# A convolution whose patches come straight out of the projection, and a scan whose states are added by identity products

## The chip, the core and the metric

The kernel runs on one core of a Trainium2 chip. The core has a matrix engine (PE, with its weight loads shown as PEld), a vector engine (DVE), an activation engine (ACT), a general engine (POOL, GpSimd) and a queueing engine (SP), which work side by side and wait for one another through semaphores; DMA engines move data. The matrix engine's clock is throttled: the profile shows the share of full speed that was granted. The metric is the device time of one execution in microseconds (us), as the median of several runs.

## The reference

Two blocks of a "metaformer" work on x of shape (2, 128, 64, 64), in float32. Each block has a token mixer and a feed-forward part, each on a normed input and with a residual. Block 0 is a deformable convolution (branches of 1x1, 1x1, 3x3, 7x7: 60 taps, each a bilinear gather) and a mixture of 8 experts. Block 1, whose mixer the change is about, is this, and ends in a mixture of 64 experts:

```
xz = einsum('ed,bdhw->behw', in_proj_w, ln_c(x))        # 128 -> 512 channels
xz = depthwise 5x5 convolution of xz, padding 2
x, z = xz[:, :256], xz[:, 256:]                          # 4096 positions each
x = sigmoid(ca(mean(x)) + ca(max(x))) * x                # channel attention
z = sigmoid(conv1d(mean and max of z over channels)) * z # position attention
x = silu(causal depthwise conv1d(x) + bias)
dt, Bm, Cm = parts of x_proj_w @ x
delta = softplus(dt_proj_w @ dt + dt_proj_b)
s[d,n]  = exp(delta*A[d,n]) * s[d,n] + delta*Bm[n]*x[d]  # scan over 4096 positions
y[d]    = sum_n s[d,n] * Cm[n] + D[d]*x[d]
out     = out_proj_w @ (y * silu(z))
```

There are 256 channels d (two halves of 128 partitions) and 16 states n.

## The kernel before, in words

**Stages and order.** On each engine the instructions run in the order in which the program issues them. The program interleaves jobs by hand: each job is a generator, its `yield` is the end of a step, and a `Side` holds a list of generators and advances the first by one step when asked. The stages are: image 0 normed; its 480 (8 groups of 512 positions by 60) gather taps, beside the offset convolutions of both images; the 480 taps of image 1, beside `after(0)`, which is image 0's norm and fusing, its first feed-forward part and its `convs(0)`; then the scan of block 1 over 16 pieces, of which the first 8 (image 0) run beside `after(1)`, the same steps for image 1; and the last feed-forward part. `sample(b, g, ..., pace)` advances the rest stream by `pace` steps per tap (L526). A scan piece is 512 positions, and one *unit* of it is one state of one half, so that a piece has 32 units; each unit advances the rest stream by five steps and a small stream `side` by two (the next piece's `prepare`, and the last one's `project`).

**The convolution, `convs(b)`.** The 512 projected channels are convolved on PE as products of patches with position matrices. The image is cut in 8 x 11 = 88 patches of 8 x 6 positions, each of which needs a halo of two: 12 x 10 = 120 values. `hs` holds the image as 11 strips (`NJ`) of 68 x 10. The steps are these:

- `norm` (L1010): a group of 512 tokens is loaded, normed, transposed on PE to `pb`, copied to `hn` by ACT (L1020) and stored to a buffer `hd` in DRAM on ACT's DMA queue (L1021).
- For each pair of channel blocks (`o`, 64 channels each), `strips` (L1025) loads every group of `hd` again on SP's queue (L1028), multiplies it with the 128 columns `own` of the projection (L1032), and copies the result into `hs` with three ACT copies (L1035, L1039, L1040).
- "ps1": for each block, 88 patches are put on partitions by a PE transpose of 64 channels x 120 positions each (L959), eight to a bank, and copied to `X` by ACT.
- "ps2": for each of the 64 channels, `X` (120 x 88) times the position matrix `tm` (120 x 48) gives the 48 outputs of all patches (L972), copied to `Y`.
- "ps3": 48 transposes (L988) bring channels back to partitions, and ACT copies them to `img`, which is stored to DRAM on SP's queue (`xsd` or `zsd`). For the z half, two reductions of `Y` on DVE (`zst`) feed the position attention.

The ACT copies are held back by two banks (`later`), and so are the stores behind them.

**The scan.** `prepare` (L1117) loads a piece of x (`xc`), of z (`zz`), of the residual (`xr`) and of the position attention (`sab`), at its start, and works out `xs` (x after conv1d), `dl` (delta), `du` (delta times x), the rows `bc` of B and C, and `dx` = D times x (L1217, ACT). For unit u the loop `scan` then runs `drive` (POOL, `db` = du times B, three units ahead, L1246), `decay` (ACT, `da` = exp, two ahead, L1253), the scan instruction (DVE, L1303), `keep` (ACT, saves the last state, L1310) and `sc` = states times C (DVE, L1313). The `sc` tile of a unit is added to `py` (one PSUM bank per half) one unit later, by four accumulating 128x128 PE transposes (L1271), so that `py` has positions on partitions. `fetch` loads the B and C rows of a state, broadcast to all partitions (512 KB), into one of `BCB` = 6 buffers (L1261). At the end of a piece, `project` copies `py` to `yt` (L1337), transposes it back (eight transposes, L104), multiplies with z (L1349), projects (L1354), adds the residual (L1364) and stores.

## Time and profile before

| | us |
|---|---|
| median of 3 runs | 8280.49 |
| lowest and highest | 8272.83, 8282.75 |
| the profiled execution | 8332.4 |
| its span, at a mean clock of 0.80 | 8330.6 |

The profile comes from one execution. Times of single instructions overlap in a pipelined engine, so a busy sum of PE isn't its time at peak. The stages, as the first and last instructions of their lines in the trace show them (us from the start of the span):

| from | to | what runs |
|---|---|---|
| 0 | 198 | norm of image 0 |
| 198 | 3093 | gathers of image 0, offset convolutions |
| 3093 | 6045 | gathers of image 1, beside `after(0)` |
| 6045 | 7435 | scan of image 0, beside `after(1)` |
| 7435 | 8055 | scan of image 1 |
| 8055 | 8330 | last feed-forward part |

The costliest rows of the groups (line, engine, operation, output<-inputs by the program's names, partitions x elements, count; then busy us, mean ns of one, idle us before and what ended it) are the gathers, their weighting and the scan's factors:

```profile
L547 POOL DMA_INDIRECT v<-table,idx x3840 | 3643.7, 949 | 2384.2 <-issue 1000.0
...
L558 DVE TENSOR_TENSOR v<-v,pw 128x1024 f32<-128x1024 f32 x960 | 1169.5, 1218 | 1060.9 <-DMA v<-table,idx 871.0
L568 PE MATMUL pst<-ident,v 128*128 128x128 f32 x7680 | 1240.2, 304 | 823.3 <-issue 529.5
...
L1246 POOL TENSOR_TENSOR db<-du,bcb 128x512 f32<-128x512 f32 x512 | 660.0, 1293 | 937.2 <-DVE da L1303 897.4
...
L1253 ACT ACTIVATE da<-delta,w_A_log 128x512 f32<-128x512 f32 x512 | 354.0, 692 | 17.3 <-DVE delta L1209 1.5
```

### The profile page before, as it was taken

The page shows a single profiled execution, that of the slowest core. Times are in us where ns is not written, and L with a number is a line of the kernel's source. Part 1 is how long each engine was busy: PE and PEld are TensorE (multiplying, and loading weights), DVE is VectorE, ACT ScalarE, POOL GpSimd, SP SyncE. Part 2 cuts the span into 40 slices and gives each one's busy share as a digit, 9 for nine tenths or more (in the row PEclk, how much of TensorE's full clock was granted, in tenths as well). Part 3 has the DMA queues.
Part 4 walks back from the last instruction along what each step waited for, and adds up shares of the span by engine and source line. Part 5 has one row for each costly group of instructions (what it writes and reads, how often), then busy time and mean ns, then how long its engine had stood idle before and what let it go on. Part 6 is the DMA issues. An engine that isn't in the chain of part 4 may idle for free. (4 is left out here: it accounts for less than half of the span.)

```text
span 8330.6 us, 83751 instructions
## 1 busy us (share of the span) xinstructions
PE 5808.5 (70%) x27808; PEld 4000.1 (48%) x27808; DVE 5729.7 (69%) x8508; ACT 2120.9 (25%) x4432; POOL 4590.5 (55%) x4576
## 2 busy tenths in 40 slices
PE   2688888888888867766766676666755565855558
PEld 2456656666666644443434443344434444733335
DVE  1577777777777776777786667666647745669981
ACT  1111111111111113211111221112163344655540
POOL 0456666666666666666666666666534433347640
PEclk7788999999999988888888888788876665656568
DMA  4677666666666668867677777777653344434434
GB/s 128 185 249 216 195 207 203 205 213 197 207 203 206 208 212 261 270 213 234 218 240 203 228 204 223 219 206 216 176 166 135 127 110 107 128 106 149 145 124 141
DMA packets 636007, 1579.35 MB, mean 190 GB/s; under 512 B 167700, under 2 KB 247356, under 8 KB 623036
## 3 DMA queue, kind: packets, MB, share of 16 engines
q0 software_dynamic: 307200, 1006.88, 40.6%
q1 hardware_dynamic: 298284, 515.10, 19.5%
q10 hardware_dynamic: 30096, 52.03, 1.7%
q8 instruction: 226, 3.70, 0.2%
q14 instruction: 201, 1.65, 0.1%
HBM read 1456.11 MB, written 120.01 MB: 189 GB/s over the span
## 5 line engine op out<-in xcount | busy, mean ns | idle before, releaser
L547 POOL DMA_INDIRECT v<-table,idx x3840 | 3643.7, 949 | 2384.2 <-issue 1000.0
L597 PE MATMUL out<-st,regw 128*128 128x512 f32 x3840 | 2115.3, 676 | 161.2 <-issue 108.7
L558 DVE TENSOR_TENSOR v<-v,pw 128x1024 f32<-128x1024 f32 x960 | 1169.5, 1218 | 1060.9 <-DMA v<-table,idx 871.0
L568 PE MATMUL pst<-ident,v 128*128 128x128 f32 x7680 | 1240.2, 304 | 823.3 <-issue 529.5
L577 ACT COPY st<-pst 128x512 f32<-128x512 f32 x960 | 558.3, 585 | 4347.3 <-remote 2367.5
L568 PEld LDWEIGHTS pst<-ident,v 128*128 128x128 f32 x7680 | 1001.1, 157 | 1162.1 <-issue 786.9
L564 DVE TENSOR_TENSOR v<-v,low 128x512 f32<-128x512 f32 x1920 | 1318.0, 686 | 65.4
L563 DVE TENSOR_TENSOR low<-v,pw 128x512 f32<-128x512 f32 x1920 | 1329.0, 692 | 33.4
L1246 POOL TENSOR_TENSOR db<-du,bcb 128x512 f32<-128x512 f32 x512 | 660.0, 1293 | 937.2 <-DVE da L1303 897.4
L597 PEld LDWEIGHTS out<-st,regw 128*128 128x128 f32 x3840 | 762.0, 221 | 776.6 <-issue 713.7
L334 PEld LDWEIGHTS po<-wout,ring 128*128 128x128 f32 x5120 | 740.1, 198 | 366.5 <-issue 365.1
L334 PE MATMUL po<-wout,ring 128*128 128x147 f32 x5120 | 785.6, 299 | 167.4 <-issue 162.3
L1303 DVE TENSOR_TENSOR_SCAN da<-da,state,db 128x512 f32<-128x512 f32 x512 | 657.1, 1283 | 278.3 <-ACT da L1253 260.8
L1271 PE MATMUL py<-ident,sc 128*128 128x128 f32 x2048 | 463.0, 379 | 336.2 <-DVE sc L1313 335.1
L1271 PEld LDWEIGHTS py<-ident,sc 128*128 128x128 f32 x2048 | 338.6, 196 | 476.8 <-DVE sc L1313 441.5
L1313 DVE TENSOR_TENSOR sc<-da,bcb 128x512 f32<-128x512 f32 x512 | 354.2, 692 | 48.6 <-DVE da L1303 1.9
L1253 ACT ACTIVATE da<-delta,w_A_log 128x512 f32<-128x512 f32 x512 | 354.0, 692 | 17.3 <-DVE delta L1209 1.5
L972 PE MATMUL ps<-tm,X 120*88 120x48 f32 x2048 | 246.1, 299 | 62.9 <-ACT Y L924 22.5
L972 PEld LDWEIGHTS ps<-tm,X 120*88 120x88 f32 x2048 | 241.7, 213 | 94.4 <-issue 41.4
L959 PE MATMUL ps<-ident,hs 64*120 64x64 f32 x1408 | 142.1, 271 | 124.9 <-ACT X L924 69.8
L988 PE MATMUL ps<-ident,Y 88*64 88x88 f32 x768 | 108.1, 291 | 155.9 <-ACT img L924 100.1
L959 PEld LDWEIGHTS ps<-ident,hs 64*120 64x120 f32 x1408 | 125.5, 177 | 184.2 <-ACT X L924 89.5
(270 smaller groups left out, 4811.1 us busy)
## 6 DMA issues: line engine op xcount, KB each, us to landing
bcb<-bc SPq DMA_DIRECT2D x256, 512.0 KB
regw<-in_regw SPq DMA_DIRECT2D x66, 1280.0 KB
v<-table,idx POOLq DMA_INDIRECT x3840
yd<-ys ACTq DMA_DIRECT2D x128, 256.0 KB
yc<-yd SPq DMA_DIRECT2D x32, 1024.0 KB
gb<-gd SPq DMA_DIRECT2D x16, 2048.0 KB
wt<-in_weight SPq DMA_DIRECT2D x32, 1024.0 KB
tm<-pos SPq DMA_DIRECT2D x16, 1440.0 KB
```

Source lines behind the costliest of these rows:

```text
L334: m()
L547: nc.gpsimd.indirect_dma_start(out=v[:, j, :], out_offset=None, in_=self.table[b], in_offset=bass.IndirectOffsetOnAxis(ap=idx[:, j, t : t ...
L558: nc.vector.tensor_tensor(up, up, w, ALU.mult)
L563: nc.vector.tensor_tensor(low, v4[:, two, 2:4, :], w, ALU.mult)
L564: nc.vector.tensor_tensor(up[:, two], up[:, two], low, ALU.add)
L568: nc.tensor.matmul(pt[:, j, :], v4[:, j, q, :], env.ident, is_transpose=True, start=j == 0 and q == 0, stop=j == GT - 1 and q == 1,)
L577: nc.scalar.copy(st, pt.rearrange("p j t -> p (j t)"))
L597: nc.tensor.matmul(self.out[half], self.regw[t // CH][:, t % CH, half * P : (half + 1) * P], st, start=first, stop=last,)
L972: nc.tensor.matmul(ps[:, c, :], X[:, c0 + c, :], tm[:, :, c0 + c], start=True, stop=True)
L1246: nc.gpsimd.tensor_tensor(dbs[u], pieces[k]["du"][:, half, :], bcb[u // 2][:, 0, :], ALU.mult)
L1271: nc.tensor.matmul(out[:, j, :], what[:, j * P : (j + 1) * P], env.ident, is_transpose=True, start=first and j == 0, stop=last and j == GT ...
L1303: nc.vector.tensor_tensor_scan(s, s, dbs.pop(u), state[:, half, n : n + 1], ALU.mult, ALU.add)
```

## The change

- `norm` no longer stores to DRAM: it copies the normed, transposed group from PSUM into `hs`, which now holds the 128 normed channels, once per image. `strips` and `hd` are gone.
- ps1 projects while it puts patches on partitions: a patch of `hs` (128 x 120) is the stationary operand, and the block's 64 columns of the projection are the moving one.
- For image 1 two blocks share one `Y`, so that ps3 transposes 88 x 128 and `img` has 128 channels (`yg`).
- `py` keeps channels on partitions: `sc` is added by one product with the identity as stationary operand, issued two units after its own; D times x is a product with a diagonal matrix `dg`, made once, issued at the piece's fourth unit. `project` then needs neither `yt` nor transposes; it runs at the head of `side` from the third unit of the next piece, and loads `xr` itself.
- Six buffers for `sc` in place of five, five for `bcb` in place of six; `zz` and `sab` load six steps later; four rest steps per unit in place of five; two rest steps per tap everywhere in place of three in group 0 of image 1.

```
-                self.sample(1, g, *cur, conv, rest, 2 if g else 3)
+                self.sample(1, g, *cur, conv, rest, 2)
...
-BCB = 6
+BCB = 5
...
-        yield from mixed([self.norm(b, g, sp, bank) for g in range(NG)], 2)
-        zst = sp.tile([NPATCH, 2, 4, NPOS], F32, name="zst", bufs=1)
+        yield from mixed([self.norm(b, g, hs, sp, bank) for g in range(NG)], 2)
+        yg = CG if b == 0 else 2 * CG
+        zst = sp.tile([NPATCH, 2, 256 // yg, NPOS], F32, name="zst", bufs=1)
         for o in range(512 // CG):
-            if o % 2 == 0:
-                own = ipw[:, o * CG : (o + 2) * CG]
-                yield from mixed([self.strips(b, g, own, hs, sp, bank) for g in range(NG)], 2)
+            ch = o * CG % yg
+            if ch == 0:
+                Y = sp.tile([NPATCH, NPOS, yg], F32, name="Y", bufs=1)
...
+            own = ipw[:, o * CG : (o + 1) * CG]
             for p0 in range(0, NPATCH, 8):
                 ps = bank([KP, 8, CG], "ps1")
                 for k in range(8):
                     i, j = divmod(p0 + k, NJ)
-                    nc.tensor.transpose(
-                        ps[:, k, :],
-                        hs[ch, j, PH * i : PH * i + PH + 4, :].rearrange("p y x -> p (y x)"),
-                        env.ident[ch, ch],
-                    )
+                    patch = hs[:, j, PH * i : PH * i + PH + 4, :].rearrange("p y x -> p (y x)")
+                    nc.tensor.matmul(ps[:, k, :], patch, own, start=True, stop=True)
...
+            if ch + CG < yg:
+                continue
...
-                    ps = bank([CG, nx, NPATCH], "ps3")
+                    ps = bank([yg, nx, NPATCH], "ps3")
...
-        nc.scalar.copy(hn, pb)
-        nc.scalar.dma_start(out=self.hd[b][:, g * 512 : (g + 1) * 512], in_=hn.rearrange("p j t -> p (j t)"))
-        yield
-
-    def strips(self, b, g, own, hs, sp, bank):
...
+        yield
+
+        pb = pb.rearrange("p j (y x) -> p (j y) x", x=W)
         rows = slice(2 + 8 * g, 10 + 8 * g)
         nc.scalar.copy(
             hs[:, 1:NJ, rows, 0:PW].rearrange("p j y x -> p y j x"),
...
+        dg = sp.tile([P, 2, P], F32, name="dg", bufs=1)
+        for h in range(2):
+            nc.vector.tensor_scalar(dg[:, h, :], env.ident, self.D[:, h : h + 1], None, ALU.mult)
...
-            for j in range(GT):
-                nc.tensor.matmul(
-                    out[:, j, :],
-                    what[:, j * P : (j + 1) * P],
-                    env.ident,
-                    is_transpose=True,
...
+            nc.tensor.matmul(py[k, half], by, what, start=first, stop=last)
...
-            if n == 0 and half == 0:
-                side.add(tail)
+            if k and n == 1 and half == 0:
+                side.todo.appendleft(project(k - 1))
...
-            sc = sp.tile([P, LC], F32, name="sc", bufs=5)
+            sc = sp.tile([P, LC], F32, name="sc", bufs=6)
...
-            for _ in range(5):
+            for _ in range(4):
                 rest.step()
...
             if n == 0 and half == 0:
-                py.clear()
-                adds.extend((h, now["dx"][:, h, :], True, False) for h in range(2))
-            adds.append((half, sc, False, n == DS - 1))
+                adds.extend((u + 3, k, h, dg[:, h, :], now["xs"][:, h, :], True, False) for h in range(2))
+            adds.append((u + 2, k, half, env.ident, sc, False, n == DS - 1))
+            while adds and adds[0][0] <= u:
+                add(*adds.popleft()[1:])
...
+    def project(self, b, k, py, ys, sp, pp):
+
+        nc = self.env.nc
+        xr = sp.tile([P, GT, C], F32, name="xr", bufs=1)
+        nc.sync.dma_start(out=xr, in_=self.x2[b][:, k * GT : (k + 1) * GT, :])
         for half in range(2):
             y = ys[:, half, :]
-            nc.vector.tensor_tensor(y, y, pts[half].rearrange("p j t -> p (j t)"), ALU.mult)
+            nc.vector.tensor_tensor(y, y, py[half], ALU.mult)
```

More of the change, by code (lines that the diff above doesn't have):

```diff
@@ L900, in __init__ @@
         self.zsd = [self.dp.tile([256, N], F32, name=f"zsd{b}", tag=f"zsd{b}") for b in range(B)]
-        self.hd = [self.dp.tile([P, N], F32, name=f"hd{b}", tag=f"hd{b}") for b in range(B)]
         self.att = [self.dp.tile([2, N + 6], F32, name=f"att{b}", tag=f"att{b}") for b in range(B)]
@@ L953, in convs @@
             X = sp.tile([KP, CG, NPATCH], F32, name="X", bufs=1)
-            ch = slice(o % 2 * CG, (o % 2 + 1) * CG)
+            own = ipw[:, o * CG : (o + 1) * CG]
             for p0 in range(0, NPATCH, 8):
@@ L966, in convs @@
             yield from last()
-            Y = sp.tile([NPATCH, NPOS, CG], F32, name="Y", bufs=1)
             for c0 in range(0, CG, 8):
@@ L974, in convs @@
                     )
-                later(copy(Y[:, :, c0 : c0 + 8], ps.rearrange("p c s -> p s c")))
+                later(copy(Y[:, :, ch + c0 : ch + c0 + 8], ps.rearrange("p c s -> p s c")))
                 yield
             yield from last()
+            if ch + CG < yg:
+                continue
             x_half = o < 4
             for py in range(PH):
-                img = sp.tile([CG, NI, W], F32, name="img", tag="io", bufs=3)
-                ch = slice((o % 4) * CG, (o % 4 + 1) * CG)
+                img = sp.tile([yg, NI, W], F32, name="img", tag="io", bufs=3)
+                at = (o + 1) * CG % 256 or 256
+                ch = slice(at - yg, at)
                 dst = self.xsd[b][ch, 3:] if x_half else self.zsd[b][ch, :]
@@ L998, in convs @@
             if not x_half:
-                nc.vector.tensor_reduce(zst[:, 0, o - 4, :], Y, AX.X, ALU.add)
+                nc.vector.tensor_reduce(zst[:, 0, (o - 4) * CG // yg, :], Y, AX.X, ALU.add)
                 yield
-                nc.vector.tensor_reduce(zst[:, 1, o - 4, :], Y, AX.X, ALU.max)
+                nc.vector.tensor_reduce(zst[:, 1, (o - 4) * CG // yg, :], Y, AX.X, ALU.max)
             yield
@@ L1007, in convs, with norm @@
         yield from self.position_attention(b, zst, sp, bank)
-    def norm(self, b, g, sp, bank):
+    def norm(self, b, g, hs, sp, bank):
         env, nc = self.env, self.env.nc
@@ L1019, in norm @@
         yield
-        nc.scalar.copy(hn, pb)
-        nc.scalar.dma_start(out=self.hd[b][:, g * 512 : (g + 1) * 512], in_=hn.rearrange("p j t -> p (j t)"))
         yield
-    def strips(self, b, g, own, hs, sp, bank):
-        nc = self.env.nc
-        h = sp.tile([P, 512], F32, name="h", tag="io", bufs=3)
-        nc.sync.dma_start(out=h, in_=self.hd[b][:, g * 512 : (g + 1) * 512])
-        for _ in range(3):
-            yield
-        pb = bank([P, 8, W], "pj")
-        nc.tensor.matmul(pb.rearrange("p y x -> p (y x)"), own, h, start=True, stop=True)
-        yield
+        pb = pb.rearrange("p j (y x) -> p (j y) x", x=W)
         rows = slice(2 + 8 * g, 10 + 8 * g)
@@ L1127, in prepare @@
         )
-        zz = sp.tile([P, 2, LC], F32, name="zc")
-        nc.sync.dma_start(out=zz, in_=self.zsd[b].rearrange("(h p) l -> p h l", p=P)[:, :, l0 : l0 + LC])
-        xr = sp.tile([P, GT, C], F32, name="xr")
-        nc.sync.dma_start(out=xr, in_=self.x2[b][:, k * GT : (k + 1) * GT, :])
-        sa = sp.tile([P, LC], F32, name="sab", bufs=1)
-        nc.sync.dma_start(out=sa, in_=self.sad[b][0, l0 : l0 + LC].partition_broadcast(P))
         def gap(n):
@@ L1138, in prepare @@
         yield from gap(6)
+        zz = sp.tile([P, 2, LC], F32, name="zc")
+        nc.sync.dma_start(out=zz, in_=self.zsd[b].rearrange("(h p) l -> p h l", p=P)[:, :, l0 : l0 + LC])
+        sa = sp.tile([P, LC], F32, name="sab", bufs=1)
+        nc.sync.dma_start(out=sa, in_=self.sad[b][0, l0 : l0 + LC].partition_broadcast(P))
         halves = range(2)
@@ L1214, in prepare @@
             yield
-        dx = sp.tile([P, 2, LC], F32, name="dx", bufs=1)
-        for h in halves:
-            nc.scalar.mul(dx[:, h, :], xs[:, h, :], self.D[:, h : h + 1])
-        res.update(dx=dx, zz=zz, dl=dl, du=du, xr=xr)
-        yield
+        res.update(xs=xs, zz=zz, dl=dl, du=du)
     def scan(self, sp, ps, pp, rest, ahead):
@@ L1238, in scan @@
         units = [(k, n, half) for k in range(B * NK) for n in range(DS) for half in range(2)]
-        pieces, das, dbs, bcb, tail = {0: res}, {}, {}, {}, iter(())
+        pieces, das, dbs, bcb = {0: res}, {}, {}, {}
         def drive(u):
@@ L1261, in fetch, with add, project @@
                 nc.sync.dma_start(out=bcb[i], in_=pieces[k]["bc"][n].partition_broadcast(P))
-        adds, py = deque(), []
-        def add(half, what, first, last):
+        adds, py = deque(), {}
+        def add(k, half, by, what, first, last):
             if first:
-                py.append(ps.tile([P, GT, P], F32, name=f"py{half}", tag=f"py{half}", bufs=1))
-            out = py[half]
-            for j in range(GT):
-                nc.tensor.matmul(
-                    out[:, j, :],
-                    what[:, j * P : (j + 1) * P],
-                    env.ident,
-                    is_transpose=True,
-                    start=first and j == 0,
-                    stop=last and j == GT - 1,
-                )
+                py[k, half] = ps.tile([P, LC], F32, name=f"py{half}", tag=f"py{half}", bufs=1)
+            nc.tensor.matmul(py[k, half], by, what, start=first, stop=last)
+        def project(k):
+            return self.project(k // NK, k % NK, [py.pop((k, h)) for h in range(2)], pieces[k]["zz"], sp, pp)
         fetch(BCB - 3)
@@ L1316, in scan @@
                 side.step()
-            for _ in range(5):
+            for _ in range(4):
                 rest.step()
-            while adds:
-                add(*adds.popleft())
             if n == 0 and half == 0:
-                py.clear()
-                adds.extend((h, now["dx"][:, h, :], True, False) for h in range(2))
-            adds.append((half, sc, False, n == DS - 1))
-            if n == DS - 1 and half == 1:
-                add(*adds.popleft())
-                yt = sp.tile([P, 2, GT, P], F32, name="yt", bufs=1)
-                tail = self.project(k // NK, k % NK, tuple(py), yt, now["zz"], now["xr"], pp)
-        for _ in tail:
-            pass
-    def project(self, b, k, py, yt, ys, xr, pp):
-        env, nc = self.env, self.env.nc
+                adds.extend((u + 3, k, h, dg[:, h, :], now["xs"][:, h, :], True, False) for h in range(2))
+            adds.append((u + 2, k, half, env.ident, sc, False, n == DS - 1))
+            while adds and adds[0][0] <= u:
+                add(*adds.popleft()[1:])
+        while adds:
+            add(*adds.popleft()[1:])
+        for _ in project(B * NK - 1):
+            pass
+    def project(self, b, k, py, ys, sp, pp):
+        nc = self.env.nc
+        xr = sp.tile([P, GT, C], F32, name="xr", bufs=1)
+        nc.sync.dma_start(out=xr, in_=self.x2[b][:, k * GT : (k + 1) * GT, :])
         for half in range(2):
-            nc.scalar.copy(yt[:, half, :, :], py[half])
-        yield
-        yield
-        pts = []
-        for half in range(2):
-            pt = pp.tile([P, GT, P], F32, name="pty", tag="m")
-            transpose4(nc, env.ident, pt, [yt[:, half, j, :] for j in range(GT)])
-            pts.append(pt)
+            y = ys[:, half, :]
+            nc.vector.tensor_tensor(y, y, py[half], ALU.mult)
             yield
         yield
-        for half in range(2):
-            y = ys[:, half, :]
-            nc.vector.tensor_tensor(y, y, pts[half].rearrange("p j t -> p (j t)"), ALU.mult)
-            yield
         po = pp.tile([P, GT, P], F32, name="po", tag="m")
```

## The prediction

> **What bounds it now.** I read the slices first, then windows cut at the stage borders (seen where L597, L1303 and L1518 begin and end), then waits and groups of each stage.

> ```profile
> PE   2688888888888867766766676666755565855558
> DVE  1577777777777776777786667666647745669981
> PEclk7788999999999988888888888788876665656568
> ```
> Read down a column: from slice 29 (6045 us) the clock falls to 5–6 tenths, while no engine is over 8 tenths busy until slice 37. The windows (us; busy us of PE, weight loads, DVE, ACT, POOL; clock; DMA share; GB/s) show three stages that the change touches: image 1's gathers (C), the first and the second half of the scan.
> ```profile
> 3093.00:6045.00 2952.00, 2019.78 (x9104) 1242.68 (x9104) 2106.53 (x3015) 571.60 (x1162) 1839.46 (x1936) 0.83 0.73 223
> 6045.00:7435.00 1390.00, 832.13 (x4564) 650.24 (x4564) 824.12 (x1107) 680.17 (x1355) 510.97 (x375) 0.64 0.41 124
> 7435.00:8055.00 620.00, 334.03 (x1337) 222.70 (x1336) 589.69 (x601) 343.96 (x674) 427.06 (x337) 0.60 0.42 142
> ```
> The second half is bound by DVE: 590 of 620. C and the first half have no full engine: instructions of two jobs stand interleaved in each engine's order, and each waits for the other. The waits of the first half (total us, times, longest):
> ```profile
> DVE da L1303 <- ACT da L1253: 260.8, 64, 21.3
> ACT state L1310 <- DVE sc L1313: 147.5, 53, 15.9
> ACT Y L924 <- PE ps L972: 100.0, 43, 11.5
> PE py L1271 <- DVE sc L1313: 81.4, 42, 7.4
> ```
> Here is a ring: the scan waits for ACT's decay, which stands behind copies of conv results; ACT waits for PE, PE waits for the scan's C product, and so back to DVE. So the convolution's PE time, and the add that holds PE, are path. All waits of this stage that end on PE come to some 290 of 1390 us: a fifth, which I use below as the share of spread-out PE time that counts.

> **How much side work each stage takes.** Counting the generators' yields: image 0's side stream has 988 steps now against 1020 offered (60 taps at 3, 420 at 2), so it lasts nearly all of C. After: the strips' 152 steps go, 836 against 960 at 2: it ends near tap 420, some 40 taps earlier than today. Image 1's stream: 1164/5 = 233 units now, 930/4 = 232.5 after: the scan is covered just as long, with 4 steps a unit in place of 5.

> **New patch products (ps1): the largest added cost.** Rows (group: count | busy, mean ns | idle before):
> ```profile
> L959 PE MATMUL ps<-ident,hs 64*120 64x64 f32 x1408 | 142.1, 271 | 124.9 <-ACT X L924 69.8
> L972 PE MATMUL ps<-tm,X 120*88 120x48 f32 x2048 | 246.1, 299 | 62.9 <-ACT Y L924 22.5
> ```
> 1408 = 16 × 88 transposes: one instruction each. L972 is a true f32 product: 1024 in the code, 2048 instructions. So the new 1408 products become 2816 instructions with 128-row loads. Means contain pipeline overlap, so I use spacing of starts: L959 0.059 us at full clock, 0.107 at half; L972 (120x48) 0.085/0.147; a 128x128 load with a short moving side (expert gate, L1518) 0.213 at half. I take 0.105/0.20 for one new instruction, two per patch: 88 × 0.21 = 18.5 us for 64 channels at full clock (35 at half) against 5.2 (9.4). Eight of these per image: **+106 us full, +206 half**.

> **Strips out.** 64 PE instructions of 128x512 (0.43/0.85 us), 96 less 24 ACT copies, 8 stores on ACT's queue and 32 loads on SP's go per image, as does the store-to-load round trip. By where L1032 runs, strips take 378 us of C (68 taps, 5.56 each) and 82 us of the scan's first half (24 units, 3.4 each). The 24 remaining copies go into norm's emptied step; the bank is held a step longer, under transposes that wait on loads anyway.

> **Stage C.** A tap costs 5.0 us by POOL's issue alone (four gathers at 0.95 plus 0.30 between them); 6.15 on average. Strips −378; the 40 bare taps come back at about 5.15 (channel statistics, a stretch with little side work, shows 5.17): +206. The finish of image 0, 60 taps at pace 3, becomes 83 at pace 2: +23 × ~5.2 = +120; norm with the strip copies and what followed the last strip: 4 taps, +21. (23 − 68 + 4 + 40: still 480 taps.) Sum −31. Then ps1: 44 taps at 5.6 today. A tap's own PE work is 2.6 (transposes 0.87, four 128x512 products 1.72); two new ps1 banks add 3.36 at full clock: 5.95, and 11.5 at half. The like stretch, ps2, is 5.3 by the same sum and took 6.85 at a clock of 0.86; so 7.2 is taken, 44 × 1.6 = +70. **C: +39**, from −15 (6.0 a tap) to +100 (8.5, less some).

> **First half.** *Strips* −32: of 82, the 24 units still cost about 2.1 each bare. *ps1*: a block of 64 channels takes 19 us today, PE's own part 7 to 8, the rest waits in the ring. After, PE bounds it: at clock 0.70, 18.5/0.70 = 26.4 us, and 14 steps at four a unit put 3.5 adds of 1.2 us between: 30.5, 8 × 11.5 = **+90**. In the same way +124 at 0.62 (today's), +177 at half, +50 at 0.85, +14 full. *ps2* follows the clock: −12 (+8 at 0.62, −40 at 0.85). *ps3 of image 1* (88x64 transposes become 88x128; 384→192 instructions, copies and DMAs 64→32, bytes unchanged): of 174 us, PE and ACT counts halve, widths don't: −49. *Adds two units later*: today add u stands on PE one unit behind its product, and ps1–ps3 behind it wait those 81 us; later, the product is long done. I take four fifths, −64; ACT's decay is late next, so not all. But an add is longer (below): 0.5 us × 204 units outside ps1 × a fifth = +20. **−44**. The sc tile is held a unit longer and has a buffer more: no new wait of DVE. *Projection*: two yt copies (ACT, 30.9 us of waits), eight pty transposes and two dx scalings per piece go: −20; D·x becomes two 512-column products. **Sum −67**, range −150 to +100.

> **Identity products against transposes[...].**
> ```profile
> L1271 PE MATMUL py<-ident,sc 128*128 128x128 f32 x2048 | 463.0, 379 | 336.2 <-DVE sc L1313 335.1
> L597 PE MATMUL out<-st,regw 128*128 128x512 f32 x3840 | 2115.3, 676 | 161.2 <-issue 108.7
> ```
> An add is four transposes, 4 × 0.109 = 0.44 us full, 0.85 half. L597 shows what it becomes: 960 taps × 2 halves are 1920 products, 3840 instructions, two each. So 0.86 full, 1.7 half. [...] The row's instruction count decides: 1.7 under 2.4, hidden by DVE, **0**. That DVE cover is 1283 + 692 ns a unit: 32 × 1.975 + 14.5 of piece work = 77.7 against 78.4 measured, and the change takes nothing from it. One y multiply per half remains. Second half 0 ± 10.

> [...] The trace is split:
> ```profile
> 6110.00:6232.00 122.00, 88.47 (x312) 57.86 (x312) 45.17 (x53) 90.92 (x179) 27.62 (x22) 0.86 0.58 186
> 7233.00:7254.00 21.00, 20.64 (x136) 20.48 (x136) 6.26 (x7) 6.16 (x14) 2.55 (x2) 0.50 0.01 2
> 8140.00:8166.00 26.00, 26.00 (x122) 25.22 (x121) 3.14 (x6) 3.51 (x6) 0.00 (x0) 0.50 0.00 1
> ```
> Wide true products (first row: 256 columns moved) stood at 0.86; but the second row is dense ps2, true products with 48 columns, and the third dense 64-column ones: both 0.50 with PE full. [...] New adds are wide and new ps1 narrow: hence 0.70.

> **Smaller edits.** BCB 6→5: a C/B row has three units' slack instead of four (about 7 us), against about 4 from issue to landing; POOL's wait on it today is 9 us. zz, sab after six steps: first used units later; xr, loaded in project with one buffer: needed five steps on. SP's queue holds only these and tm, img. Cost 0; if the cover fails, up to 1 us for each of 128 rows.

> **Rivals.**
> (1) *The clock doesn't rise* (slower). ps1's 64-column products run slow like the third row above, beside a scan at 0.60. First half: +124 +8 −32 −49 −20, and adds at half clock −64 + 0.85 × 204 / 5 = −29: +2; C at 7.7 a tap: +61; tail −3: +60, **8340**. It decides when the first half's clock stays below about 0.67. For: dense ps2 at 0.50. Against: the wide adds.
> (2) *It rises to 0.85*: +50 −40 −32 −49 −50 −20 = −141, C −10: **8130**. [...] Against: 0.50.
> (3) *Parts cancel*, clock near 0.67: **8280**.
> (4) *Late prefetch*: 1 us a row in the second half, +128, on −30: **8378**.

> **Numbers.** C +39, first half −67, second 0, tail −3 (shorter last projection): −31. Durations come from an execution of 8332.4 us (span 8330.6), 0.6% over the median of 8280.5; 0.6% of 31 is nothing, so it is taken from the median: **8250**. Chances: forecast 0.38, rival 1 0.36, rival 2 0.08, rival 3 0.13, rival 4 0.05. 0.2% (16.6 us) is what can be told from no change: faster 0.46, same 0.13, slower 0.41. The forecast's own range is 8180 to 8262; with the others 8150 to 8370.

> **What will show it.** Strips (L1032, h loads) gone; ps1 spacing near 0.105/0.20 and two instructions a patch; clock 6045–7435 at 0.70 or more (rival 1: 0.62 or under); PE's wait for sc under 30 us; second half 620 ± 10 with PE near 1.7 a unit[...]; C some 2990 us, with 40 bare taps at its end. The forecast is wrong if C grows over 100 us or the first half doesn't shrink.

## The result, and the profile after

The changed kernel takes 8164.42 us in the median of 4 runs (8158.65 to 8199.58), the kernel before 8278.98 (8272.83 to 8282.75): ratio 0.9871, 95% interval 0.9842 to 0.99. So it is 1.3% faster, some 115 us where 31 were forecast. The profiled execution took 8158.65 us (span 8156.9).

The profiled execution of before took 8332.4 us, 0.6% over its median and longer than any of its timed runs, and part of that lies where the change touches nothing: image 0's taps lasted 2894 us in it and 2867 after. Chips differ in this stretch in the runs below too (2863 to 2872 on one, 2898 to 2912 on the others). So a difference of stage lengths between two traces holds such a part too, and verdicts rest on ratios to the kernel before, run on the same chip.

First the slices of after (a column is 204 us):

```profile
PE   2588888888888875767776886887556677956668
PEclk9789999989999987978888888888777787877788
```

Against the rows shown of before: the clock stands at 7 to 8 tenths from slice 29 on, where it had been 5 to 6. The windows of the three stages (columns as before: us, busy PE, weight loads, DVE, ACT, POOL, clock, DMA, GB/s), and two short ones, the last ps1 block and the last ps2 block of image 1:

```profile
3098.00:5951.00 2853.00, 2027.41 (x9618) 1306.13 (x9616) 2081.71 (x2983) 538.34 (x1068) 1817.12 (x1913) 0.84 0.72 223
6012.00:7267.00 1255.00, 882.91 (x4402) 582.32 (x4402) 807.43 (x1093) 597.38 (x1156) 495.50 (x364) 0.78 0.40 123
7267.00:7881.00 614.00, 406.70 (x728) 137.37 (x728) 588.35 (x599) 329.58 (x643) 425.89 (x337) 0.77 0.43 144
7092.00:7112.00 20.00, 20.00 (x180) 19.03 (x179) 7.06 (x8) 8.64 (x17) 6.89 (x6) 1.00 0.57 153
7113.00:7126.00 13.00, 13.00 (x134) 11.88 (x134) 4.98 (x6) 4.89 (x11) 3.82 (x3) 1.00 0.01 1
```

The taps are taken by their weighting (L558), the scan from one scan instruction (L1303 before, L1286 after) to another. So taken, the stages are:

| | before | after | difference |
|---|---|---|---|
| taps of image 0 (unchanged code) | 2894 | 2867 | −27 |
| taps of image 1 | 2907 | 2853 | −55 |
| scan, first half | 1351 | 1255 | −96 |
| scan, second half | 617 | 613 | −4 |

The first half holds most of it; what image 1's taps are worth is taken up below. Second half and tail are where the prediction put them: PE's busy time went from 334 to 407 us of some 615 in the second half, hidden by DVE. In the first half PE has *more* busy time than before (883 against 827, from the first scan instruction on) in a shorter stage. The last two rows of the fence say how: PE, full in ps1 for 20 us, stood at a clock of 1.00, and so did ps2, which had stood at 0.50 in the same place before. The groups:

```profile
L1258 PE MATMUL py<-sc,ident 128*128 128x512 f32 x1024 | 646.2, 747 | 227.8 <-DVE sc L1296 226.5
...
L962 PE MATMUL ps<-ipw,hs 128*120 128x64 f32 x2816 | 341.8, 285 | 32.7 <-ACT X L924 20.5
...
L970 PE MATMUL ps<-tm,X 120*88 120x48 f32 x2048 | 190.3, 265 | 18.7 <-issue 8.6
```

1408 patches are 2816 instructions and 512 adds 1024: two each, as the prediction had read from rows of before. ps2, which nobody edited, went from 246 to 190 us busy in the whole kernel.

### The profile page after: what moved, and what is told of

It reads as the page before. It is cut to its first block, busy times and chain, and to the rows that moved or that the text cites. A ratio compares the mean times of both kernels' runs of the same rounds, so it can differ in the third digit from the quotient of the medians.

```text
span 8156.9 us, 82968 instructions
## 1 busy us (share of the span) xinstructions
PE 5965.2 (73%) x27680; PEld 3939.3 (48%) x27680; DVE 5724.5 (70%) x8506; ACT 2015.3 (25%) x4142; POOL 4590.3 (56%) x4576
## 5 line engine op out<-in xcount | busy, mean ns | idle before, releaser
L597 PE MATMUL out<-st,regw 128*128 128x512 f32 x3840 | 2076.0, 665 | 137.9 <-issue 78.8
L558 DVE TENSOR_TENSOR v<-v,pw 128x1024 f32<-128x1024 f32 x960 | 1169.2, 1218 | 1039.7 <-DMA v<-table,idx 850.7
L568 PE MATMUL pst<-ident,v 128*128 128x128 f32 x7680 | 1219.1, 302 | 753.6 <-issue 404.4
L597 PEld LDWEIGHTS out<-st,regw 128*128 128x128 f32 x3840 | 750.8, 218 | 741.5 <-issue 666.3
L334 PE MATMUL po<-wout,ring 128*128 128x147 f32 x5120 | 802.8, 301 | 218.3 <-issue 215.5
L1286 DVE TENSOR_TENSOR_SCAN da<-da,state,db 128x512 f32<-128x512 f32 x512 | 656.8, 1283 | 239.9 <-ACT da L1242 232.1
L1258 PE MATMUL py<-sc,ident 128*128 128x512 f32 x1024 | 646.2, 747 | 227.8 <-DVE sc L1296 226.5
L1258 PEld LDWEIGHTS py<-sc,ident 128*128 128x128 f32 x1024 | 200.2, 224 | 553.8 <-DVE sc L1296 422.8
L962 PEld LDWEIGHTS ps<-ipw,hs 128*120 128x120 f32 x2816 | 342.1, 202 | 79.2 <-ACT X L924 39.3
L962 PE MATMUL ps<-ipw,hs 128*120 128x64 f32 x2816 | 341.8, 285 | 32.7 <-ACT X L924 20.5
L970 PEld LDWEIGHTS ps<-tm,X 120*88 120x88 f32 x2048 | 185.9, 168 | 52.9 <-issue 26.3
L334 PE MATMUL po<-wring,ring 128*128 128x174 f32 x1024 | 187.4, 323 | 23.8 <-issue 22.9
L970 PE MATMUL ps<-tm,X 120*88 120x48 f32 x2048 | 190.3, 265 | 18.7 <-issue 8.6
```

The costliest lines, as they stand in the source:

```text
L334: m()
L558: nc.vector.tensor_tensor(up, up, w, ALU.mult)
L568: nc.tensor.matmul(pt[:, j, :], v4[:, j, q, :], env.ident, is_transpose=True, start=j == 0 and q == 0, stop=j == GT - 1 and q == 1,)
L597: nc.tensor.matmul(self.out[half], self.regw[t // CH][:, t % CH, half * P : (half + 1) * P], st, start=first, stop=last,)
L962: nc.tensor.matmul(ps[:, k, :], patch, own, start=True, stop=True)
L1258: nc.tensor.matmul(py[k, half], by, what, start=first, stop=last)
```

## The experiments

Theory 1 after the result: the gain is the clock, 0.78 in the first half where it was 0.64, and the change's true products raise it. 1a says that the wide adds do it, 1b that ps1's narrow products suffice. Theory 2, the rival: the gain is the removed work (strips, copies, projection), and the clock a by-product. The first four runs take the change apart. "Ratio" is always to the kernel before on the same chip, with its 95% interval.

**The scan part alone.** The scan of the changed kernel put into the kernel before:

```
-            for j in range(GT):
-                nc.tensor.matmul(
...
-                    is_transpose=True,
...
+            nc.tensor.matmul(py[k, half], by, what, start=first, stop=last)
...
-            adds.append((half, sc, False, n == DS - 1))
+            adds.append((u + 2, k, half, env.ident, sc, False, n == DS - 1))
```

> The kernel before with the scan part of the change alone (identity products two units later, dg, project at the head of side, later loads of zz, sab, xr; buffers for C/B rows stay at six, steps at five). If the wide true products are what raises the PE clock (theory 1a): clock of the first scan half from 0.64 to 0.72 or more, ps2 there partly at full clock, first half 50 to 80 us shorter, gather stage unchanged; about 8210 to 8230. If the gain comes from the work that the convolution lost (theory 2): clock as before, first half 0 to 40 us shorter by the adds' later issue and the shorter projection; about 8240 to 8280.

Measured: 8351.74 against 8338.06 us, ratio 1.0018 (1.0004 to 1.0031); first half 1380 us at a clock of 0.70, ps2 still mostly at 0.50. Both expectations of a gain fall. Later issue, shorter projection and a warmer clock together bring nothing here.

**The convolution part alone**: the changed kernel with the old scan put back (four steps a unit and five C/B buffers stay), and without the shared Y. Against the changed kernel:

```
-        yg = CG if b == 0 else 2 * CG
+        yg = CG
...
-            nc.tensor.matmul(py[k, half], by, what, start=first, stop=last)
+            for j in range(GT):
+                nc.tensor.matmul(
...
+                    is_transpose=True,
```

> The changed kernel with the scan of before (transposing adds one unit later, dx on ACT, yt copies) and without the shared Y (it does not fit beside the old scan's tiles); four steps a unit, five C/B buffers. If narrow true products in ps1 suffice to raise the clock (theory 1b): ps1 and ps2 of the first scan half near full clock, first half 40 to 80 us shorter and the gather stage 20 to 50 shorter; about 8180 to 8220. If only wide products raise it (1a): ps1 of the scan half at about half clock, 30 us and more per block in place of 19 to 22, first half +50 to +120 longer; about 8300 or more. If removed work makes the gain (theory 2): the gather stage and the first half each 20 to 60 us shorter with the clock as before.

Measured: 8384.3 us, ratio 1.0061 (1.0041 to 1.008). First half 1368 us at 0.65, second half 652. It is what theory 1a and the prediction's slower rival describe, but not throughout. Windows of this run's trace: the first half, then two ps1 blocks of it:

```profile
6077.00:7444.00 1367.00, 913.00 (x5192) 771.62 (x5192) 809.14 (x1097) 626.57 (x1245) 503.46 (x361) 0.65 0.38 113
7182.00:7220.00 38.00, 38.00 (x193) 38.00 (x192) 16.38 (x16) 14.63 (x24) 6.34 (x5) 0.50 0.35 98
7306.00:7326.00 20.00, 19.85 (x190) 19.71 (x189) 15.30 (x12) 9.48 (x21) 7.60 (x6) 1.00 0.77 201
```

The same instructions, with PE full in both: one block ran at half clock to its end, the other at full clock to its end. Of eight blocks, five took 35 to 38 us, one 28, two 21 to 22. Dense narrow products left the clock where they found it, in one block for 38 us. It rose inside two of the blocks (the one of 28 us and one of 35), each time behind 8 to 12 transposing instructions of the scan.

**True adds in the kernel before**: one line taken out, so that the four 128-column transposes of an add are four true products with the identity.

```
-                    is_transpose=True,
```

> The kernel before with one word less: the four 128-column adds of a unit are true products with the identity (same result, twice the PE instructions, same order). Theory 1[...]: clock of the first half 0.70 or more, of the second above 0.70 in place of 0.60, and in spite of twice the PE work 20 to 70 us faster; about 8210 to 8260. Theory 2 (work alone counts): clock as before, 0.85 us a unit more on PE in the first half at half clock, a fifth of it path: 20 to 50 us slower; about 8300 to 8330.

Measured: 8362.64 us, ratio 1.0047 (1.0029 to 1.0065). The clock did rise, to 0.71 and 0.81 in the two halves (theory 1), and the time didn't fall (theory 2). First half 1372 us; ps1 and ps3 are still transposes here, and five of the eight ps2 stretches stood at 0.50 throughout.

**True products in ps1 of the kernel before**, on 64 channels as its strips have them, transposing only:

```
-                    nc.tensor.transpose(
+                    nc.tensor.matmul(
                         ps[:, k, :],
                         hs[ch, j, PH * i : PH * i + PH + 4, :].rearrange("p y x -> p (y x)"),
                         env.ident[ch, ch],
+                        start=True,
+                        stop=True,
                     )
```

> The kernel before with ps1's 64x120 transposes as true products with the identity (same result, 2 instructions a patch in place of 1, strips kept). If narrow true products raise the clock (theory 1b): ps2 of the first scan half at 0.8 or more in place of 0.50, first half 20 to 50 us shorter; about 8230 to 8260. If they don't (1a or theory 2): ps1 blocks twice as long on PE at half clock, 9 us more a block, 30 to 70 us slower in the first half and up to 30 in the gather stage; about 8310 to 8380.

Measured: 8553.38 us, ratio 1.026 (1.0243 to 1.0277). Blocks of 33 to 44 us at 0.50 to 0.62; first half 1508 us, image 1's taps 2974. It is worse than the 30 to 100 us expected: the narrow products alone are slow and cold, so 1b falls. Five of the eight blocks had full clock at or near their start and lost it within 4 to 8 us of it.

Each half of the change, alone, is slower than before: the first by 0.3% at most, and the second without the shared Y. What makes their sum faster is the question of the next runs, of which the first is the changed kernel again, as a control.

> The changed kernel itself again, on the chip of the runs beside it. If the chips differ only by a factor: ratio 0.985 to 0.989. If its gain hangs on where the clock happens to stand (the theory after the first four runs: narrow true products of 128x64 keep whatever clock they find, so that a run can fall to half clock in ps1), executions scatter more than those of the kernel before, by up to 100 us, and ps1 blocks of 38 us stand beside such of 21.

Measured: 8173.19 us (8165.61 to 8188.43), ratio 0.9888 (0.9862 to 0.9914); before 8274.97 on this chip. The first half is as in the first trace (1252 us, clock 0.78); image 1's taps took 2873 us, 20 more than there. It scatters no more than before does, so the good clock isn't luck.

**The convolution part with true adds**: the second run above and the one line of the third, and nothing else of the scan part.

> The convolution part alone (its ps1 blocks took 35 to 38 us at half clock and 21 to 22 at full, ratio 1.006) with the old adds turned into true 128-column products, and nothing else of the scan part. Theory C (the gain is an interaction through the clock: true adds between narrow products lift it): ps1 blocks 21 to 25 us, clock of the first half 0.75 or more, first half 60 to 110 us under that of the convolution alone, about 0.990 to 0.997 of before (its second half keeps the 35 us of C/B waits). Theory D (what was missing is the later issue of the adds and the shorter projection): blocks stay at 35 and more, ratio 1.006 or above.

Measured: 8231.97 us, ratio 0.995 (0.9934 to 0.9965), where the convolution part alone had 1.0061: one line, without a change of order or of bytes and with more PE instructions, is worth 1.1%. The first half fell from 1368 to 1275 us, its clock rose from 0.65 to 0.80, and of the eight blocks six took 22 to 24 us, two 34 and 36. Theory C holds and D falls. PE's timeline (start, us, instruction, count) shows 64 ps1 instructions in the convolution part alone (first fence) and in this run (second):

```profile
7103.00 1.12 PE L1261 MATMUL py<-ident,sc 128*128 128x128 f32 x4
7103.90 12.91 PE L962 MATMUL ps<-ipw,hs 128*120 128x64 f32 x64
```
```profile
7103.93 2.00 PE L1261 MATMUL py<-ident,sc 128*128 128x128 f32 x16
7105.77 6.83 PE L962 MATMUL ps<-ipw,hs 128*120 128x64 f32 x64
```

12.91/64 is 0.202 us an instruction, 6.83/64 is 0.107: the two spacings of the prediction. In the changed kernel the rise can be seen in one block, the one behind the channel attention, where PE had been idle for over half of the 100 us before it:

```profile
6961.44 2.02 PE L1258 MATMUL py<-sc,ident 128*128 128x512 f32 x2
6963.26 12.91 PE L962 MATMUL ps<-ipw,hs 128*120 128x64 f32 x64
6975.96 2.02 PE L1258 MATMUL py<-sc,ident 128*128 128x512 f32 x2
6977.78 5.77 PE L962 MATMUL ps<-ipw,hs 128*120 128x64 f32 x48
6983.38 1.08 PE L1258 MATMUL py<-sc,ident 128*128 128x512 f32 x2
```

Two adds at half clock (2.02 us), 64 narrow instructions at half clock between them; after the second add 48 of them take 5.77, and the next add 1.08. After the first add the clock stayed at 0.50; after the second it stood at 1.00.

What goes ahead of a rise can be counted in the traces of the kernel before and of the changed kernel. Each record of the clock in them says 0.50 or 1.00, and 1200 of the 1202 records last a whole multiple of 3.413 us, so both spans were cut into pieces of that length along the clock's records. For each piece, the columns of PE's instructions (64 for one of 128x64) were added up, each instruction spread evenly over its record and weighted by its rows as a share of 128. Of 1620 pieces with under 1450 such columns, none was followed by a piece at full clock; of 3001 with over 1600, all were; of the 145 between, 60. One boundary for all 4766 is at its best wrong for 24. Without the weighting by rows the best is wrong for 105. Without the columns of transposes it is wrong for 458: in these two traces transposes go with the clock as true products do. In the kernel before, 18 of the 302 rises follow a piece in which PE ran only transposes. Here is one of them (1566 weighted columns), first in PE's timeline, then as the piece that held it and the next one (columns of the fence as above):

```profile
7260.82 1.97 PE L988 MATMUL ps<-ident,Y 88*64 88x88 f32 x12 [0.25 <-ACT img L924]
7262.59 1.06 PE L1271 MATMUL py<-ident,sc 128*128 128x128 f32 x4
7263.44 1.97 PE L988 MATMUL ps<-ident,Y 88*64 88x88 f32 x14
```
```profile
7261.00:7264.30 3.30, 3.30 (x22) 3.25 (x22) 3.27 (x3) 2.80 (x8) 0.87 (x2) 0.50 0.52 134
7264.40:7267.70 3.30, 2.40 (x25) 1.90 (x23) 3.19 (x3) 1.72 (x5) 3.21 (x3) 1.00 0.90 213
```

The blocks agree with these counts. In the block of the changed kernel above, a piece of narrow instructions alone held 1092 columns at half clock, where one came every 0.202 us, and one at full clock after the second add, where one came every 0.107, held 2061: the first is among the pieces that full clock never followed, the second among those that it always did. Three pieces of 1092 stood in a row at half clock (6965.4 to 6975.7 us). A transposing add among them brings 512 columns in 0.85 us, an estimate of some 1320 a piece at half clock from these spacings; a true one is two instructions for each of a transpose and brings 1024 in 1.82 us, by the same estimate some 1530, if one piece holds all of it. Counted for the two adds above: 1466, the first add being cut by a border between pieces, and half clock after it; 1569, and full clock after it. So what the one line adds is columns, and it takes no other difference between true products and transposes to account for it. An example of the rows: in the kernel before, the piece from 6895.75 us moved 2560 columns at full clock, most of them by instructions of 64 and of 8 rows, so that they weigh 1088, and was followed by half clock. The products of the fourth run have 64 rows too.

**Adds one unit later instead of two**, in the changed kernel:

```
-            adds.append((u + 2, k, half, env.ident, sc, False, n == DS - 1))
+            adds.append((u + 1, k, half, env.ident, sc, False, n == DS - 1))
```

> The changed kernel with its adds one unit later, as before, in place of two (D x at the third unit). Prediction: the later issue is worth about 64 us of waits, so 20 to 60 us slower, ratio to before 0.990 to 0.995, and PE's wait for sc in the first half up by 40 us or more. If the clock alone made the gain: within 10 us of the changed kernel.

Measured: 8175.99 us, ratio 0.9883 (0.9857 to 0.9909); the control has 0.9888. The later issue is worth nothing in sum: here the first half is 1239 us and the second 624, against 1255 and 613. PE's wait for sc in the first half, here and then in the changed kernel:

```profile
PE py L1258 <- DVE sc L1296: 85.4, 38, 14.8
```
```profile
PE py L1258 <- DVE sc L1296: 65.5, 30, 12.1
```

It does shrink by 20 us, but the first half is no shorter for it.

**Without the shared Y; five or six buffers.** Two runs of the changed kernel with `yg = CG`, the first with `BCB = 6`:

> The changed kernel without the shared Y of image 1 (64 channels a time in ps3), its room used for the sixth C/B buffer. Predicted worth of the shared Y: 49 us; POOL's wait for C/B rows in the first half (140 us, 18 times) should go to under 20. If the wait is path: 20 to 60 us faster than with five buffers, so the sum within 30 us of the changed kernel; if it is hidden behind the scan's own wait for ACT: 40 to 50 us slower than the changed kernel.

> The changed kernel without the shared Y (64 channels a time in ps3 for image 1 too), five C/B buffers kept. The run with six buffers and no shared Y was 0.4% (32 us) slower than the changed kernel. If the sixth buffer brought something there, this one is slower still, by 20 to 40 us more (ratio to before 0.995 to 0.998); if the waits for C/B rows in the first half cost nothing, it stands at the same ratio, 0.992 to 0.994, and the whole 32 us are the shared Y's.

Measured: 8205.6 us, ratio 0.9927 (0.9902 to 0.9953), with six; 8283.93, ratio 0.9923 (0.99 to 0.9947), with five. With the sixth buffer POOL's wait for C/B rows is gone from the first half's list of waits, where the changed kernel's has

```profile
POOL db L1235 <- DMA bcb<-bc: 139.7, 18, 18.0
```

and the time is the same: this wait is hidden. The shared Y is worth 0.35% to 0.4%, some 30 us; the first half is 1289 and 1299 us without it, against 1252 and 1255 with it.

**The old step counts** in the changed kernel:

```
-            for _ in range(4):
+            for _ in range(5):
                 rest.step()
```

(and three per tap in group 0 of image 1).

> The changed kernel with the step counts of before: five rest steps a unit, three per tap in group 0. Image 1's side stream then ends after some 186 units in place of 232, so that 46 more units run bare (2.4 us), and each covered unit holds a quarter more work. By the additive view (work decides, units don't): within 15 us of the changed kernel. If a unit's own waits add to its side work: 20 to 80 us faster with fewer covered units. In the gather stage the stream ends near tap 390 and group 0's taps are longer: plus 0 to 20 us.

Measured: 8351.37 us over 20 runs, ratio 1.0004 (0.9991 to 1.0018). The whole gain is gone, against both expectations. The first half is split here near the end of image 1's stream, where the last copy of its position attention is issued (its position weights run on beside four or five more units): the changed kernel, then this run:

```profile
6012.00:7170.00 1158.00, 819.82 (x4312) 565.81 (x4312) 745.86 (x1032) 539.32 (x1062) 448.16 (x326) 0.78 0.41 125
7170.00:7267.00 97.00, 63.09 (x90) 16.52 (x90) 61.57 (x61) 58.06 (x94) 47.34 (x38) 0.71 0.31 103
```
```profile
6105.00:7269.00 1164.00, 804.29 (x4178) 577.72 (x4178) 623.56 (x925) 495.20 (x957) 368.11 (x268) 0.75 0.37 112
7269.00:7476.00 207.00, 141.28 (x224) 43.16 (x224) 164.29 (x169) 110.71 (x203) 120.96 (x96) 0.71 0.36 117
```

The stream takes 1158 us with 230 units inside it and 1164 with 184. A unit inside costs next to nothing; the 46 that no longer fit run behind it, for 110 us more. The same split of before has 1256 us with 231 units, and 95 us behind it. A part of the loss can lie in the gather stage, whose step count was set back too: image 1's taps took 2917 us here, and 2882 in the run with five buffers and no shared Y on the same chip.

**Warmer still.** ps3's transposes, and then also those of norms, inputs and gates, as true products:

```
-                        nc.tensor.transpose(ps[:, x, :], Y[:, py * PW + x0 + x, :], env.ident[:NPATCH, :NPATCH])
+                        nc.tensor.matmul(ps[:, x, :], Y[:, py * PW + x0 + x, :], env.ident[:NPATCH, :NPATCH], start=True, stop=True)
```

> The changed kernel with ps3's transposes (88x128 in image 1, 88x64 in image 0) as true products with the identity: twice their instructions. Theory C[...]: clock of the first half from 0.775 to 0.80 or more, the ps1 blocks of 25 to 36 us (those after ps3) near 22, 0 to 30 us faster than the changed kernel. If ps3 is limited by ACT's copies and its added PE work only delays them: 0 to 30 us slower.

> As the run before, with the transposes of the norms, the projections' inputs and the gates' as true products too (not those of the gathers). Theory C: first half's clock 0.82 or more and its feed-forward stretch (326 us in the changed kernel) 10 to 40 us shorter; the gather stage shorter by up to 30. Against it: these stretches wait for ACT and DVE, not for PE, so that a warm clock brings nothing: within 15 us of the run before.

Measured: ratios 0.9917 (0.9892 to 0.9942) and 0.9938 (0.9918 to 0.9958), both above the control's 0.9888, the second clear of noise. The clock of the first half stayed at 0.77 and the half took 1278 and 1295 us. More true products are no end in themselves. That ACT's copies set the pace in these stretches, so that they are only more PE work, fits this but isn't shown. No version here beats the changed kernel clear of noise.

## Why the prediction was right, and where it was off

The direction held, and 8164 lies in the wide range of 8150 to 8370; it lies under the forecast's own range, 8180 to 8262. The size didn't hold: −31 against −115. Rival 2 (8130, given a chance of 0.08) came nearer than the forecast's 8250. The likely place, the first half, was right; that its sum of −67 came near the −96 is in part luck, since terms that failed upwards and downwards offset one another. By its own terms:

- **The clock in the first half.** Taken at 0.70, granted 0.78. Rival 2 took 0.85; the prediction weighed its wide products at 0.86 against two dense rows at 0.50 and concluded that narrow products run cold. In the traces of before and after it is the columns that go with the clock, transposes included (one boundary is wrong for 24 of 4766 pieces, without the transposes for 458), and true adds move twice the columns of the transposing ones, 1024 against 512. The rows at 0.50 were right readings of stretches that began at half clock; their pieces moved 1045 to 1308 weighted columns (7233 to 7254 us) and 1023 to 1493 (8140 to 8166).
- **ps1, first half: +90.** Its eight blocks took 201 us against 155, +46. The spacing (0.105/0.20) was right, the clock off.
- **ps2: −12.** 115 us against 161, −46, by the clock: six of its eight blocks stood at 0.50 throughout before, none after.
- **Strips: −32.** 82 us went entirely. The prediction let "24 units cost about 2.1 each bare" remain; but by its own count of steps as many units stay covered as before (230, 231), so none was bared.
- **Finish and feed-forward part of image 1: priced at nothing.** The stretch ahead of the convolution grew from 612 to 647 us. With five steps a unit it was 626, so more than half of it seems to come with the slower step rate.
- **Adds later: −44.** Zero, as shown by their undoing. The waits of 81 us were read as path because PE stood in the ring. The share of a fifth was also read too low: the waits of this stage that end on PE come to 446 us in the trace, a third of it, and not 290.
- **Shared Y: −49.** 37 to 44 us in the first half's traces, some 30 by ratio: right in kind, a little too large.
- **Projection, yt, dx: −20.** Not seen in the first half: the convolution with true adds and the old projection had 1275 us there, with the new scan part 1289 and 1299.
- **Gather stage: +39.** The traces show −55, but 27 or so of it is the difference in image 0's untouched taps, and the control has 20 us more than the first trace. On one chip, the old convolution took 2897 and 2887 us (first and third run) and the new one 2892 (second). So the stage hardly changed, and most of the 115 us lies in the scan's first half. The term that failed is ps1's "+70": 66 taps at 5.60 us, where before had 69 at 5.59. The prediction put two banks into each of 44 taps, 5.95 us of PE a tap; with the held copies' steps a block spreads over 8.25 taps, 2.6 + 18.5/8.25 = 4.8 us, less than a tap lasts.
- **Second half: 0.** −4, with the adds at two instructions each; an add takes 0.91 us at full clock in the timeline. The prediction's 0.86 was near, and at half clock an add took 1.82, under the half's 2.4 us a unit (620 us over 256 units).
- **Signs.** PE's wait for sc was to fall under 30 us, and is 65.5. The clock (0.78), the two instructions a patch and the second half (613 us) came as forecast.
- **Step counts: no change in cover.** Right, and more weighty than the prediction said. With the stream 98 us shorter (1256 to 1158), the count decides whether this is gained: with the old counts all of it is lost, most of it to units that run behind the stream.
- **Rival 1** is what the convolution part does alone, and ps1 on 64 channels still more; **rival 4**'s prefetch stall appears in the two runs with five buffers and the old order of loads: second half 652 and 650 us, with POOL waiting for C/B rows (30 and 43 us). With the loads of zz, sab and xr moved and five buffers it is 613, with six and the old order 617. That the moved loads alone are the cure is likely but wasn't isolated.

Two things stay open: why the scan part alone gains nothing, though its clock rose, and how far fewer steps a unit could go. By the count, three would need 930/3 = 310 units, more than the 252 before the drain, so only a value between could gain part of the 97 us behind the stream; it wasn't tried.

## What to carry to other kernels

Price an edit of TensorE work together with the clock that it leaves behind: two parts that each lose alone (1.0018 and 1.0061) gained 1.1 to 1.3% together, because the true adds of one stand among the other's narrow products: in the changed kernel a piece of those alone held 1092 columns at half clock, one with an add 1569, and the clock stood at 1.00 after it. Here a side stream covered a main loop, its length set the stage's, and the loop's units in it were next to free; so after shortening such a stream, spread it over as many units as before, or the gain goes to units that run bare. A wait of 81 us inside a ring was worth nothing here: undo such a wait in a test before adding it to a sum.
